# Twenty TensorE transpositions of the identity ahead of the first token tile

## The chip, the cores and the metric

The kernel runs on one core of a Trainium2 chip. A time is the device time of one execution in microseconds (us). The kernel before was timed three times: 1539.28, 1539.81 and 1539.98, median 1539.81. A fourth execution was recorded by the hardware profiler; all durations below are from it. PE is TensorE (matrix products and transpositions), PEld its weight loads, DVE is VectorE, ACT is ScalarE, POOL is GpSimd, SP is the engine that issues most DMAs.

## The reference

Eight sequences of 512 tokens with 512 features go through one block:

```python
xn = layernorm(x)
q, k, v = (xn @ W.T + b for W, b in ((Wq, bq), (Wk, bk), (Wv, bv)))
context = (elu(q) + 1) * cumsum((elu(k) + 1) * v, axis=1) * 32 ** -0.5
s = context @ Wo.T + bo
h = fwht(xn * SU_ug) / 64
h = silu(h @ W_gate.T * wg * 64) * (h @ W_up.T * wu * 64)
g = silu((fwht(h * SU_dp) / 64) @ W_down.T * wd * 64)
out = x + s * g
```

`fwht` is a normalized Walsh-Hadamard transform over the features; there are 2048 hidden features.

## The kernel before

The eight sequences are taken as four pairs. All matrices are float32. Every big product is a 2 by 2 block product done with seven products in place of eight; the seven operands are named P1 to P7, and their token side lies in one tile, `xo`, whose seven places are made by subtractions on DVE. The Hadamard transforms are folded into the weights on the chip, a first time through, by DVE butterflies and a PE product with the matrix `had` (tiles `pw`, `pwd`).

The first pair is special. Its token tiles x come in row by row, and `first_layernorms` (lines 157 to 185) normalizes eight tiles of 128 tokens: for each, DVE takes statistics (L173, L174) and adds epsilon (L175), ACT takes the root into `rs_first` (L176), DVE takes the reciprocal (L180), and then ACT scales the tile (L183, first four tiles) or DVE does (L185, last four). `transposed` (L271 to L289) then turns each tile with four PE transpositions into a PSUM bank `pt` (L276). For the first sequence ACT copies the bank into places P1 and P2 of `xo` (L280). For the second, ACT copies half of it into P3 (L283), and DVE makes P5, P6 and P7 from the bank and from places that are there already (L284 to L286). The bank pool has two buffers with the tag `t`, used in turn, so the third tile's transpositions wait until the first tile's bank has been read.

The products follow: `group` (L469) accumulates P1, P6, P5 and P3 in a bank px, P2 in py and P7, P4 in pz. For k of the first pair these are px_k with P1, py_k, px_k with P6, pz_k with P7, and so on. ACT takes snapshots of px (L481), and DVE adds (L485). The weights w_k, w_v, w_q are encoded in the same manner by DVE (L321 to L324) after their four parts have landed (L363), and are stored for later pairs (L335). The output projection uses w_o (loaded by L380), banks px_o, py_o, pz_o (L545).

The order on each engine is not the source's. A list scheduler with its own idea of how long instructions take, and with priorities in program order, places instructions one by one; each engine then works through its list strictly in order. Only the DVE part of `first_layernorms` is pinned in program order. So an instruction that is added ahead changes what the scheduler believes to be ready, and with that the order of others.

## Time and profile before

| what | value |
|---|---|
| median of three timed runs | 1539.81 us |
| profiled execution, its own time | 1539.19 us |
| its span, first to last instruction | 1537.4 us |
| PE busy | 1519.2 us (99%) |
| DVE busy | 1001.7 us (65%) |
| ACT busy | 419.6 us (27%) |
| first PE instruction | 7.22 us after the start |
| PE waits over 0.5 us after that | 2.17, 1.0, 0.65 and 0.63 us |

A line in a timeline gives the start, the duration, the engine, the source line, the operation, output and inputs, the count, and in brackets how long the engine was idle before it and what ended that. A line in the chain of waits gives the start, how long it set the pace, and what it was. In a table by stretches, each engine has its busy time and, in brackets, its number of instructions; the last three columns are the granted TensorE clock, the share of DMA and GB/s. The record of the granted clock starts with its first change, so stretches ahead of that show 1.00 whatever the clock was.

### The profile page before, as it was taken

To read this page: it belongs to the slowest core of one execution; us is meant where nothing else is said; L and a number is where in the kernel's file an instruction comes from. 1 tells how busy PE (TensorE), PEld (TensorE's weight loads), DVE (VectorE), ACT (ScalarE), POOL (GpSimd) and SP (SyncE) were. 2 spreads that over 40 slices of the span, in tenths; PEclk is the share of its full clock that TensorE was granted. 3 is DMA by queue.
4 is the path that set the end of the run, shared out by engine and by line. 5 is a ranking of instruction groups with operands and counts; after the bars stand their busy time and mean duration, and the time that the engine had idled before them with its cause. 6 is when DMAs were issued, how large, how long until landed. Compare 5 with 4: busy or idle time off the path is not lost.

```text
span 1537.4 us, 15667 instructions
## 1 busy us (share of the span) xinstructions
PE 1519.2 (99%) x5924; PEld 1121.8 (73%) x5924; DVE 1001.7 (65%) x1471; ACT 419.6 (27%) x664; POOL 345.0 (22%) x188
## 2 busy tenths in 40 slices
PE   7999999999999999999999999999999999999998
PEld 3446446748864688888884588888886478888887
DVE  8999787579775765426867674716675575633673
ACT  4462442232135311112114421111213431111211
POOL 1000000001221161107320153303611126200631
PEclk9999999999999999999999999999999999999999
DMA  8345888698965235254675344344574233525462
GB/s 283 94 142 178 265 276 252 215 321 276 273 236 145 100 119 188 86 193 147 198 268 191 88 165 151 106 143 166 195 235 152 72 120 107 191 93 179 163 257 82
DMA packets 197692, 273.31 MB, mean 178 GB/s; under 512 B 56816, under 2 KB 155120, under 8 KB 193392
## 3 DMA queue, kind: packets, MB, share of 16 engines
q1 hardware_dynamic: 197472, 272.27, 54.0%
q8 instruction: 47, 0.77, 0.2%
q14 instruction: 29, 0.24, 0.0%
q10 hardware_dynamic: 144, 0.03, 0.0%
HBM read 196.25 MB, written 76.02 MB: 177 GB/s over the span
## 4 chain that ended last, share of the span: by engine, by line
PE 92%; DVE 5%; DMA 1%; ACT 1%; issue 1%; POOL 0%; SPq 0%; POOLq 0%; DVEq 0%; ACTq 0%
PE px_gu L647 20%; PE px_dn L545 14%; PE pz_gu L647 10%; PE pz_dn L545 7%; PE py_gu L647 5%; PE py_dn L545 4%; PE px_o L545 3%; PE px_k L469 3%; PE px_q L469 3%; PE px_v L469 3%; PE px_gate L469 2%; PE px_up L469 2%; PE pz_o L545 2%; PE pz_v L469 2%; PE pz_k L469 2%; PE pz_q L469 2%
## 5 line engine op out<-in xcount | busy, mean ns | idle before, releaser
L647 PE MATMUL px_gu<-xo,w_gu 128*128 128x256 f32 x1456 | 347.4, 380 | 0.0
L647 PEld LDWEIGHTS px_gu<-xo,w_gu 128*128 128x128 f32 x1456 | 276.1, 190 | 43.9 <-issue 5.0
L545 PE MATMUL px_dn<-w_down,ho 128*128 128x256 f32 x1024 | 228.8, 379 | 1.0 <-DVE ho L93 1.0
L856 POOL TENSOR_TENSOR u<-u,v 128x1024 f32<-128x1024 f32 x26 | 61.2, 2374 | 721.7 <-DVE u L685 682.4
L545 PEld LDWEIGHTS px_dn<-w_down,ho 128*128 128x128 f32 x1024 | 194.6, 190 | 29.3 <-issue 1.9
L647 PE MATMUL pz_gu<-xo,w_gu 128*128 128x256 f32 x728 | 187.3, 380 | 0.0
L647 PEld LDWEIGHTS pz_gu<-xo,w_gu 128*128 128x128 f32 x728 | 137.8, 190 | 20.2 <-DVE a L689 0.9
L545 PE MATMUL pz_dn<-w_down,ho 128*128 128x256 f32 x496 | 112.4, 379 | 0.0
L545 PEld LDWEIGHTS pz_dn<-w_down,ho 128*128 128x128 f32 x496 | 93.9, 190 | 14.5 <-issue 1.2
L647 PE MATMUL py_gu<-xo,w_gu 128*128 128x256 f32 x364 | 93.4, 379 | 0.0
L901 POOL TENSOR_TENSOR s<-s,d 128x512 f32<-128x512 f32 x30 | 40.0, 1333 | 165.5 <-ACT d L900 165.5
L647 PEld LDWEIGHTS py_gu<-xo,w_gu 128*128 128x128 f32 x364 | 69.2, 190 | 9.4
L860 POOL TENSOR_TENSOR v<-v,r 128x1024 f32<-128x1024 f32 x26 | 60.8, 2362 | 27.2 <-DVE r L685 27.2
L469 PE MATMUL px_k<-xo,w_k 128*128 128x512 f32 x128 | 61.1, 600 | 0.0
L846 ACT ACTIVATE a<-a,cols_sb 128x512 f32<-128x512 f32 x26 | 18.7, 721 | 154.3 <-DVE a L685 152.7
L469 PE MATMUL px_v<-xo,w_v 128*128 128x512 f32 x128 | 60.6, 594 | 0.0
L469 PE MATMUL px_q<-xo,w_q 128*128 128x512 f32 x128 | 60.3, 592 | 0.0
L900 ACT ACTIVATE d<-d 128x512 f32<-128x512 f32 x31 | 19.5, 630 | 144.4 <-DVE d L560 124.7
L545 PE MATMUL px_o<-w_o,co 128*128 128x256 f32 x256 | 58.5, 380 | 0.2 <-DVE sa_o L556 0.2
L846 ACT ACTIVATE u<-u,cols_sb 128x512 f32<-128x512 f32 x52 | 36.9, 720 | 78.2 <-DVE u L685 75.0
L545 PE MATMUL py_dn<-w_down,ho 128*128 128x256 f32 x256 | 57.9, 379 | 0.0
L841 POOL TENSOR_TENSOR ho<-ho 128x1024 f32<-128x1024 f32 x24 | 56.3, 2355 | 1.4
(264 smaller groups left out, 2282.5 us busy)
## 6 DMA issues: line engine op xcount, KB each, us to landing
w_gu<-d_gu SPq DMA_DIRECT2D x91, 896.0 KB, 4.4
w_down<-d_down SPq DMA_DIRECT2D x56, 512.0 KB, 4.0
d_s<-o SPq DMA_DIRECT2D x8, 1024.0 KB, 6.0
d_d<-dn SPq DMA_DIRECT2D x8, 1024.0 KB, 7.6
d<-d_d SPq DMA_DIRECT2D x8, 1024.0 KB, 5.8
s<-d_s SPq DMA_DIRECT2D x8, 1024.0 KB, 7.7
y<-in_x_dram SPq DMA_DIRECT2D x8, 1024.0 KB, 6.9
out_dram<-y SPq DMA_DIRECT2D x15, 512.0 KB, 3.3
```

The lines of the kernel that those rows point to most:

```text
L469: nc.tensor.matmul(p.rearrange("p a t -> p (a t)") if len(r.shape) == 2 else p, ws[k][:, i, :], r, start=(first and k == 0), stop=(k == n ...
L545: nc.tensor.matmul(p[:, c], t[:, (2 * g + c) * P : (2 * g + c + 1) * P], ws[i](k), start=(first and k == 0 and c == cs[0]), stop=(k == n - ...
L647: nc.tensor.matmul(p[:, lane], w[:, lane, i, :], x[:, i, :], start=(first and lane == 0), stop=True, skip_group_check=True,)
L841: eng.tensor_tensor(ho[:, :, c], ho[:, :, a], ho[:, :, b], ALU.subtract)
L846: nc.scalar.activation(g[:, m], g[:, m], AF.Silu, scale=col("w_gate", u + m * NU + a * NG))
L856: nc.gpsimd.tensor_tensor(r[:, m], ru1[:, m], rv[:, m], ALU.add)
L860: nc.gpsimd.tensor_tensor(rv[:, m], rv[:, m], rr[:, m], ALU.add)
L900: nc.scalar.activation(d, d, AF.Silu)
L901: (nc.vector if final and (a, s) == (1, 0) else nc.gpsimd).tensor_tensor(r, r, d, ALU.mult)
```

## The change

After the identity matrix has been made, a PSUM tile `spare` with the tag `t` is taken, and PE transposes the identity into it twenty times. Nothing reads `spare`. The output does not depend on it. Since `spare` takes a buffer of the pool `t`, the first token tile's bank is now the other of the two.

```diff
     nc.scalar.dma_start(cols_sb, cols)
     make_identity(nc, ident)
+    spare = ps.tile([P, P], F32, tag="t", name="spare")
+    for _ in range(20):
+        nc.tensor.transpose(spare, ident, ident)
     had2 = t8.tile([P, P], F32, tag="t", name="had2")
```

## The prediction

> **What bounds the kernel now.** I read the page first, then the list of what PE waited for, then the chain of waits, then stretches of the first and last microseconds.

> ```profile
> span 1537.4 us, 15667 instructions
> ...
> PE   7999999999999999999999999999999999999998
> ```

> The list of PE's waits (who, for whom, total us, times, longest):

> ```profile
> PE pt L276 <- ACT x L183: 7.2, 1, 7.2
> PE pz_o L545 <- DVE g L485: 2.2, 1, 2.2
> PE px_dn L545 <- DVE ho L93: 1.0, 1, 1.0
> PE pz_k L469 <- DVE k L485: 0.2, 1, 0.2
> ```

> PE is the bound in all slices but the first and last, and its waits after the first 7.2 us are few. So whatever PE loses or gains in the first 23 us arrives at the end, unless one of those waits takes it up. The start itself, from the chain (start, how long it set the pace, what):

> ```profile
> 10.95 0.48 ACT xo L280
> 11.42 0.04 issue
> 11.47 1.97 PE pt L276 x8
> 13.44 2.39 PE px_k L469 x4
> 15.83 0.44 PE pt L276 x4
> 16.27 1.72 PE py_k L469 x4
> ...
> 23.16 1.92 PE px_k L469 x4
> ```

> Until 11.47 us the normalization on DVE and ACT sets the pace, then PE. Eight transpositions take 1.97 us there (1.79 from first start to the next product's start at 13.26, so 0.22 each); later four take 0.44, 0.11 each. The change of pace falls inside the first px_k, at about 14.5 us: before it PE ran at half speed. I call that the closed clock. The rows by stretches say when it opens and closes:

> ```profile
> 7.60:11.00 3.40, 2.63 (x12) 1.74 (x10) 3.12 (x13) 3.15 (x7) 0.00 (x0) 1.00 1.12 355
> 11.00:14.40 3.40, 3.23 (x12) 2.19 (x11) 3.36 (x12) 2.05 (x6) 0.00 (x0) 1.00 1.02 302
> ...
> 1530.00:1533.40 3.40, 1.62 (x8) 1.09 (x6) 2.69 (x6) 1.04 (x2) 0.00 (x0) 1.00 0.45 175
> 1533.40:1536.80 3.40, 0.00 (x0) 0.00 (x0) 0.87 (x3) 0.42 (x1) 0.00 (x0) 1.00 0.57 210
> 1536.80:1537.40 0.60, 0.00 (x0) 0.00 (x0) 0.00 (x0) 0.00 (x0) 0.00 (x0) 0.52 0.00 0
> ```

> PE busy is the first figure after the comma. A stretch with 2.63 of 3.40 busy did not open the clock, one with 3.23 did; one with 1.62 at the end did not close it, an empty one did (0.52 after 1536.8). So a nearly full stretch opens, and the share that closes lies somewhere between 0 and 48%.

> **The change, part by part.** All sums are against the profiled execution, 1539.19 us, which is 0.62 below the median of 1539.81.

> *The twenty transpositions.* They wait for the identity alone (POOL, done at 1.30). At 0.22 us each they end by 1.3 + 20 x 0.22 = 5.7 us. The first token tile is ready at 7.12, when PE starts at 7.22 in the profile. They cost nothing directly; the cover is this wait of 7.2 us, and without it they would cost 2.2 (open) to 4.4 us (closed).

> *The bank.* `spare` takes one of two buffers, and only PE writes it. The second token tile takes it over in PE's own order, so there is no new wait; the banks alternate as before. Zero.

> *The order on ACT and PE.* This is the part with a price. The changed program's order (where its instructions stand, not when) shows that the scheduler believes the token tiles to be turned later and puts ACT's copies (L280) behind more of the normalization. ACT had copy 0, scale 3, copy 1, root 5, copies 2 and 3, root 6. It will have scale 3, root 5, copy 0, root 6, copies 1, 2, 3, root 7. DVE's order is the same up to the last statistics. Root 6 is the trap, as these two rows show:

> ```profile
> 11.42 0.58 ACT L280 COPY xo<-pt 128x512 f32<-128x512 f32 x1
> ...
> 13.05 0.14 DVE L175 TENSOR_SCALAR rs_first<-mv_first 128x1 f32<-128x1 f32 x1
> ```

> Copies 1 and 2 began at 10.85 and 11.42; now they stand behind root 6, which needs the DVE result of 13.05 + 0.14. By the rows' durations: root 5 at 11.1, copy 0 to 11.85, root 6 13.25 to 13.45, copy 1 to 13.95, copy 2 to 14.45. PE turns tile 3 in the bank of copy 1 from 14.0, ACT copies it, PE turns tile 5 in that bank, and only then comes px_k, because PE's list now has tiles 4 and 5 ahead of it. With the clock open: tile 3 to 14.45, copy 3 from 14.6 to 15.2, tile 5 from 15.25 to 15.7, px_k from 15.7 to 17.4. Before, px_k plus the same six tiles were done at 16.1. Next, PE's list is py_k, tiles 6 and 7, px_v, half of py_v: 1.72 + 0.88 + 1.72 + 0.86 = 5.18, so px_k's second product starts at 22.6. DVE, which makes P6 for it, gets there at about 22.5: the root of tile 7 comes earlier (it stood behind the px_k snapshot, a DVE wait of 0.66 at 16.95), and four encodings of w_v move into that hole. In the profile this product started at 23.1, but with two half-products of 0.86 more behind it. So PE loses 22.6 + 1.72 - 23.1 = 1.2 us by order alone.

> *The clock at px_k.* It would have to be opened by the twenty (4.4 us dense) and stay open over the poor stretch that follows: tiles 0 to 2 at 7.2, 8.45 and 11.9, each 0.44, tile 3 at 14.0. A stretch of 3.4 us there holds about 0.44, or 13%. The rows leave 0 to 48% open; 13% is nearest to the empty row, which closed. I take it as closed. Then tile 3 takes 0.85, copy 3 runs 15.1 to 15.7, tile 5 ends at 16.6, and px_k starts 0.9 later than above. From 16.6 until the opening g, PE does half its work: (g - 16.6)/2. The bounds of g: the dense work began at 11.47 in the profile and opened 3.0 later, so 14.0 + 3.0 = 17.0; or from PE's first instruction, 7.3 us, so 14.0 + 7.3 = 21.3. The opening also came only 1.2 us after the first matrix product (13.26), so the row can't say if transpositions count; by that count g is 17.8. I take 18.5, nearer the dense row: 0.95 us.

> [...]

> *What takes it up or adds.* The PE wait of 0.2 us for k (67.5) goes: -0.2. The wait of 2.2 us of pz_o does not help, since the chain runs through PE to it:

> ```profile
> 102.28 1.73 PE px_gate L469 x4
> 104.01 0.20 SPq L380
> ...
> 105.61 3.71 DMA w_o<-in_wo_t_dram
> ```

> PE frees the weight buffer at 104.0, w_o lands at 109.3, DVE had waited 2.0 us for it and is busy from there to 134.8. If PE is late at 104, all of it is late. In the new order two 256-wide px_o products (0.43 together, as eight of py_o took 1.73) move from ahead of that wait to behind it: +0.43. The wait of 1.0 us at 240 hangs on pw_up of PE at 218 through two transfers, so it moves along.

> *SP, ACT and DVE later.* The store of w_k moves ahead of the last load of the next w_k, which lands some 1.5 us later, for a reader at 25.0 (its landing takes 4.0): hidden. The second load of rd moves behind the store of w_v; its reader is at 40.8. The load of bo_r moves ahead of w_v's second load by 0.4 us of issue. Around 170 us the store to wd_f moves behind two loads, and one of eight reads back (0.7 us of issue) ahead of the s_up stores; rd is read at 190.6. sa_up moves behind two groups of pwd scalings on ACT, whose product px_up moved as well. POOL's order is the same. I put all these at zero; uncovered, each would cost up to its issue, 0.4 to 0.7 us.

> Sum: 1.2 + 0.9 + 0.95 - 0.2 + 0.43 = 3.3, so 1539.19 + 3.3 = 1542.5 us, 0.17% over the median.

> **The rivals.**

> *Open at px_k.* The twenty open the clock and 13% keeps it open. 1.2 - 0.2 + 0.43 = 1.4: 1540.6 us. For it: 48% kept it open. Against: a stretch of 13%.

> *Late opening: slower.* One mechanism, the clock opening at px_k and after. The base with opening at 16.6 is 1539.19 + 1.2 + 0.9 - 0.2 + 0.43 = 1541.5; 1542.9 is passed if g is over 19.3, and 21.3 gives 1543.9; its middle, 20.3, gives 1543.4. It decides if only matrix products count and the stretches fall badly.

> *The change does what it says: faster.* Clock open and the copies no trap: 4.36 us of the chain (1.97 + 2.39) would be 0.88 + 1.72 = 2.60, so 1.76 less, 1537.4. To pass 0.2% the wait of 2.17 us must go too: 1535.3. Against it: P6 on DVE was ready only at 23.1 anyway, and the order above.

> **How the numbers follow.** About 0.2% (3.1 us) is what a measurement can tell from no change. Closed with g up to 19.3: 0.38, no change. Open: 0.22, no change. Late opening: 0.35, slower. A gain past 0.2%: 0.05. So 0.05, 0.60 and 0.35. The range goes from 1540.2 (the open case less 0.4 for a moved transfer) to 1544.2 (g of 21.3 plus 0.3).

> **What would show it.** In the profile after: 20 transpositions between 1.3 and 5.8 (right if PE's first wait shrinks to 1.3); copy 1 of L280 after 13.3; px_k from 15.7 (open) or 16.6 (closed); four transpositions taking 0.85 or 0.44 at 14.0; px_k's second product at 22.6 or later; the wait of pz_o at 136 to 139 with about 2 us. If the copies are not late, or the pz_o wait shrinks by a microsecond, the sum is wrong.

## The result and the profile after

The changed kernel took 1543.28 us (median of 22 executions, 1540.84 to 1544.36), the kernel before on the same chip 1539.49 (22 executions). The ratio is 1.002, with a 95% interval of 1.0014 to 1.0026: slower by about 3 us by the ratio, while the medians lie 3.79 apart. The executions of the changed kernel fall into two groups, twelve from 1543.18 to 1544.36 with a mean granted clock of 0.995 and ten from 1540.84 to 1542.60 with 0.996 to 1.0; both profiles of it, here and in the repeated run below, are of the upper group. The profiled execution took 1543.74 us, 4.55 more than that of before (1539.19). The page of the changed kernel:

```profile
span 1542.0 us, 15704 instructions
...
PE   8999999999999999999999999999999999999998
...
PEclk8999999999999999999999999999999999999999
```

PE's first digit is 8 in place of 7, since the twenty transpositions fill the old wait, and the clock's first digit is 8 in place of 9. The list of PE's waits (who, for whom, total us, times, longest):

```profile
PE pt L276 <- ACT xo L280: 3.7, 2, 2.7
PE pz_o L545 <- DVE g L485: 2.2, 1, 2.2
PE pt L276 <- ACT x L183: 2.0, 2, 1.4
PE spare L1162 <- POOL ident masks.py:199: 1.4, 1, 1.4
...
PE px_dn L545 <- DVE ho L93: 0.5, 1, 0.5
```

The first wait of 7.2 us has become 1.4 and 1.4 us, and a new one stands at the top: 3.7 us in which PE waits for ACT's copies. The timeline shows it (start, duration, engine, line, operation, output and inputs, count; in brackets the idle time before and what ended it):

```profile
1.36 4.39 PE L1162 MATMUL spare<-ident 128*128 128x128 f32 x20 [1.36 <-POOL ident masks.py:199]
...
7.11 0.66 PE L276 MATMUL pt<-ident,x 128*128 128x128 f32 x4 [1.36 <-ACT x L183]
...
11.81 1.12 PE L276 MATMUL pt<-ident,x 128*128 128x128 f32 x4 [2.74 <-ACT xo L280]
...
13.18 0.20 ACT L176 ACTIVATE rs_first<-rs_first 128x1 f32<-128x1 f32 x1 [1.42 <-DVE rs_first L175]
13.29 1.05 ACT L280 COPY xo<-pt 128x512 f32<-128x512 f32 x2
...
13.91 2.91 PE L276 MATMUL pt<-ident,x 128*128 128x128 f32 x12 [0.98 <-ACT xo L280]
...
16.61 3.14 PE L469 MATMUL px_k<-xo,w_k 128*128 128x512 f32 x4
```

Copies 1 and 2 begin at 13.29, right behind root 6 at 13.18; px_k begins at 16.61 in place of 13.26. The first four transpositions of a token tile take 0.66 us, those at 11.81 take 1.12: the clock was open and closed again. The table by stretches (busy time of PE, PEld, DVE, ACT, POOL with instructions in brackets, then granted clock, DMA share, GB/s):

```profile
5.40:8.80 3.40, 1.42 (x11) 0.92 (x9) 3.09 (x16) 2.24 (x6) 0.52 (x2) 1.00 1.05 367
8.90:12.30 3.40, 0.66 (x5) 0.50 (x4) 3.19 (x12) 2.40 (x5) 0.00 (x0) 0.50 1.15 343
12.30:15.70 3.40, 2.42 (x12) 1.79 (x11) 3.40 (x15) 1.80 (x5) 0.00 (x0) 0.50 0.50 147
15.70:19.10 3.40, 3.40 (x8) 1.92 (x8) 3.39 (x11) 0.79 (x3) 0.00 (x0) 0.50 0.97 283
...
135.10:138.50 3.40, 1.23 (x6) 0.78 (x5) 3.40 (x4) 0.50 (x1) 0.00 (x0) 1.00 1.15 344
138.60:142.00 3.40, 3.40 (x10) 2.69 (x9) 3.40 (x7) 0.55 (x1) 0.00 (x0) 0.50 0.09 28
```

The trace's record of the clock has it open from 5.48 us, half from 8.89, open from 19.13, and then, which the prediction did not have, half again from 138.59 to 142.01. These changes and the closing at the end (1541.47) lie multiples of 3.413 us apart: 1, 4, 39, 40 and 450 times 3.413 behind the first. I call such a stretch of 3.413 us a window. In before, the clock opened at 14.48 us and stayed open until 1536.82, 446 times 3.413 later and behind PE's last product.

Where the 4.55 us come from can be followed on PE, by the start of the same matrix product in both profiles. At px_k's second product PE starts at 24.75, 1.64 later than before (23.11), with 1.72 us of products moved behind it: 3.36 us late. At pz_o behind the wait of 2.17 us it is 138.02 against 135.55, 2.47 late, with four px_o products of 0.86 moved behind it: 3.33. From 145 us on, where the order is nearly the same, PE is 5.01 late: the second closing has added 1.68. The wait of px_dn at 240 us gives 0.47 back, since it is 0.5 in place of 1.0. That leaves 4.54.

### The profile page after: what moved, and what is told of

Read it like the earlier page. It is cut to its first block, busy times and chain, and to the rows that moved or that the text cites. A ratio compares the mean times of both kernels' runs of the same rounds, so it can differ in the third digit from the quotient of the medians.

```text
span 1542.0 us, 15704 instructions
## 1 busy us (share of the span) xinstructions
PE 1524.9 (99%) x5944; PEld 1126.4 (73%) x5944; DVE 1003.3 (65%) x1471; ACT 420.1 (27%) x664; POOL 345.1 (22%) x188
## 4 chain that ended last, share of the span: by engine, by line
PE 91%; DVE 5%; DMA 1%; ACT 1%; issue 1%; POOL 0%; SPq 0%; POOLq 0%; DVEq 0%; ACTq 0%
PE px_gu L647 20%; PE px_dn L545 14%; PE pz_gu L647 10%; PE pz_dn L545 7%; PE py_gu L647 5%; PE py_dn L545 4%; PE px_o L545 4%; PE px_k L469 3%; PE px_v L469 3%; PE px_q L469 3%; PE px_gate L469 2%; PE px_up L469 2%; PE pz_o L545 2%; PE pz_k L469 2%; PE pz_v L469 1%; PE pz_q L469 1%
## 5 line engine op out<-in xcount | busy, mean ns | idle before, releaser
L545 PE MATMUL px_dn<-w_down,ho 128*128 128x256 f32 x1024 | 228.8, 379 | 0.5 <-DVE ho L93 0.5
L545 PEld LDWEIGHTS px_dn<-w_down,ho 128*128 128x128 f32 x1024 | 194.5, 190 | 29.0 <-issue 1.9
L647 PEld LDWEIGHTS pz_gu<-xo,w_gu 128*128 128x128 f32 x728 | 137.7, 190 | 20.3 <-DVE a L689 0.9
L545 PE MATMUL pz_dn<-w_down,ho 128*128 128x256 f32 x496 | 112.4, 379 | 0.0
L545 PEld LDWEIGHTS pz_dn<-w_down,ho 128*128 128x128 f32 x496 | 93.8, 190 | 14.6 <-issue 1.2
L469 PE MATMUL px_k<-xo,w_k 128*128 128x512 f32 x128 | 61.7, 605 | 0.0
L469 PE MATMUL px_v<-xo,w_v 128*128 128x512 f32 x128 | 60.4, 594 | 0.0
L469 PE MATMUL px_q<-xo,w_q 128*128 128x512 f32 x128 | 60.1, 592 | 0.0
L545 PE MATMUL px_o<-w_o,co 128*128 128x256 f32 x256 | 59.0, 381 | 0.0
L545 PE MATMUL py_dn<-w_down,ho 128*128 128x256 f32 x256 | 57.9, 379 | 0.0
```

What stands on the lines that cost most here:

```text
L469: nc.tensor.matmul(p.rearrange("p a t -> p (a t)") if len(r.shape) == 2 else p, ws[k][:, i, :], r, start=(first and k == 0), stop=(k == n ...
L545: nc.tensor.matmul(p[:, c], t[:, (2 * g + c) * P : (2 * g + c + 1) * P], ws[i](k), start=(first and k == 0 and c == cs[0]), stop=(k == n - ...
L647: nc.tensor.matmul(p[:, lane], w[:, lane, i, :], x[:, i, :], start=(first and lane == 0), stop=True, skip_group_check=True,)
```

## The experiments

All the experiments but the changed kernel itself fix the order. A helper of 39 lines gives each engine a list of the positions of its first instructions (205 on ACT, 327 on DVE, 116 on SP, 291 on PE) and chains them by dependences for the scheduler alone, without a wait on the chip. The list is that of before ("early") or that of the changed kernel ("late"). With the helper, L280 is L319, L469 is L508 and L545 is L584. Its core:

```diff
+    for engine, places in ORDER.items():
+        mine = [i for i in bb.instructions if i.engine.name == engine and i.name not in extra ...]
+        chain = [mine[p] for p in places]
...
+        for i, j in zip(chain[1:], chain):
+            tc.add_manual_dep(i, j.name, DependencyInfo(NoSync, DATA), reason="as_listed")
```

### The order without the twenty, and the twenty without the order

Theory: the new order costs, the transpositions themselves are free. Rival: the transpositions cost, through the clock or the bank. The first kernel has the late lists and no transpositions:

```diff
     make_identity(nc, ident)
-    spare = ps.tile([P, P], F32, tag="t", name="spare")
-    for _ in range(20):
-        nc.tensor.transpose(spare, ident, ident)
...
+    as_listed(tc, extra, ())   # ORDER: the changed kernel's
```

> The lists of all engines are those of the changed kernel, but the twenty transpositions are left out. Theory O (the order costs, the twenty themselves do nothing lasting): copy 1 (L280) begins after 13.2 us, px_k at about 16.6 us with the clock closed, its second product at 24.3 to 25.2 us in place of 23.1, and the time is that of the changed kernel within 1 us, 1542 to 1544. Theory C (the clock that the twenty open and lose again costs, the order little): without them the clock opens as before at 14.5 to 17 us, and the time is 1539.5 to 1541.

Measured: 1543.77 us against 1540.07 of before on that chip, ratio 1.0022 (1.0013 to 1.0031). The whole loss is there without a single added transposition. px_k begins at 16.67, its second product at 24.11, a little ahead of the 24.3 to 25.2 that was expected:

```profile
16.67 2.43 PE L508 MATMUL px_k<-xo,w_k 128*128 128x512 f32 x4
```

The second has the twenty and the early lists:

```diff
+    spare = ps.tile([P, P], F32, tag="t", name="spare")
+    for _ in range(20):
+        extra.add(nc.tensor.transpose(spare, ident, ident).ins.name)
...
+    as_listed(tc, extra, ())   # ORDER: that of before
```

> The twenty transpositions, with all engines' lists as in the kernel before. Theory O: the twenty open the clock at 5 to 8 us and lose it again, px_k begins at 13.3 us or earlier, its second product at 23.1 us within 0.4, time 1539.5 within 0.7. Theory C: the clock lost at about 9 us opens later than the 14.5 us of before, and the time is 1541 to 1542.

Measured: 1539.84 us, ratio 0.9999 (0.999 to 1.0008). The twenty cost nothing, and they gain nothing: in the profile they open the clock at 4.76 us, it closes at 8.17 and opens again at 15.00, half a microsecond later than in the profile of before, and px_k begins at 13.27. Two of the eleven executions lie higher, at 1542.55 and 1543.57, with a mean clock of 0.995 where the other nine have 0.997 or 0.998; they have no profile.

### One instruction put back

The changed kernel, with only root 6 moved in ACT's list behind copies 1, 2 and 3:

```diff
-    "Activation": [..., 10, 13, 11, 14, 15, 16, 12, 17, ...],
+    "Activation": [..., 10, 13, 14, 15, 16, 11, 12, 17, ...],
```

> The changed kernel with one instruction moved on ACT: root 6 behind copies 1, 2 and 3 in place of ahead of them. If root 6 is what makes the copies late: copy 1 at 11.8 us, px_k at about 15.2 us in place of 16.6, time 1541 to 1542.2. If the cost lies in PE's list (tiles 4 and 5 ahead of px_k): 1543 to 1543.7 as before the move.

Measured: 1540.18 us, ratio 1.0004 (0.9996 to 1.0013), below both of the expected ranges. One root of 128 numbers, moved by three places, takes back most of the loss: nearly all of it by the median, and all but some 0.6 us by the ratio. Six of the eleven executions lie at 1539.91 to 1540.18, the other five 2 us higher, at 1542.05 to 1542.25; the profile is of the lower group, and why the five are slower is not shown. The table by stretches and the timeline of this kernel show how:

```profile
12.30:15.70 3.40, 3.40 (x18) 2.80 (x17) 3.40 (x15) 1.49 (x6) 0.00 (x0) 0.62 0.67 179
15.70:19.10 3.40, 3.37 (x12) 1.34 (x10) 3.40 (x12) 1.59 (x4) 0.00 (x0) 1.00 0.96 276
```

```profile
11.88 3.44 PE L315 MATMUL pt<-ident,x 128*128 128x128 f32 x16 [2.31 <-ACT xo L319]
...
15.16 1.88 PE L508 MATMUL px_k<-xo,w_k 128*128 128x512 f32 x4
```

PE turns four tiles without a gap from 11.88 on, so one window is nearly full (2.98 of 3.41 us busy) and the clock opens at 14.86, ahead of px_k. In the changed kernel the gap until 13.91 breaks that window (2.42 of 3.40 us busy in the stretch from 12.30); the clock opens only at 18.39 to 19.13 in its two profiles, and most of px_k runs in the closed clock.

### The clock held open, order of before

Can the clock be worth something by itself? Here transpositions fill PE's gaps from 1.4 us to px_k, with the early lists:

```diff
-    for _ in range(20):
-        nc.tensor.transpose(spare, ident, ident)
+    spare = bank("px", "spare", 2)[:, 0, :P]
+    for ahead_of, n in ((0, 28), (4, 6), (8, 10), (12, 6)):
+        filler(ahead_of, n, spare)   # n transpositions ahead of PE's listed instruction
```

> Lists as in the kernel before, with 28 transpositions of the identity ahead of tile 0 and 6, 10 and 6 more behind tiles 0, 1 and 2, so that PE has no poor stretch before px_k. If the closed clock at the start has a price on the path: open from 8.2 us at the latest without closing, px_k at 12.6 us and done by 14.4, 1538.4 to 1539.0. If DVE sets the second product of px_k anyway: it stays at 23.1 us and the time at 1539.5. If the fillers get in the way of the tiles: 1540 or more.

Measured: 1539.15 us, ratio 0.9994 (0.9985 to 1.0003). In the profile, of the fastest of the eleven executions (1537.91), PE is 1.03 us ahead of before at px_k's second product and from 145 us on. The same kernel once more on another chip:

> The order of the kernel before with the clock held open from 7 us through px_k, once more: the only kernel so far below the kernel before (1539.15 against 1540.07, ratio 0.9994 with an interval that holds 1). Theory C (px_k in the open clock gains 1.03 us at 25 us and nothing takes it up): 0.8 to 1.3 us below the kernel before, the load of w_gate at 242 us takes 3.2 us, and PE waits for nothing at 246 to 253 us. Rival D (the gain is lost to a slower load of w_gate at 242 us, as in the kernel with both fillings, where it took 5.3 us and PE waited 2.2): within 0.5 us of the kernel before or above it, with a wait of pz_dn at about 251 us.

Measured: 1540.83 us against 1540.85, ratio 1.0 (0.9991 to 1.0009). In this profile PE is 0.71 us ahead at px_k's second product, but the clock closes for a window at the wait of pz_o (135.77 us), and from 145 us on PE is 1.01 late. So there is a gain at px_k in the profiles, and no kernel here that can be told from before to its good.

### The second closing

First the changed kernel once more:

> The changed kernel once more, on the chip of the next three. All theories: 3 to 4 us over the kernel before, in two groups some 2.3 us apart, the lower one with a mean clock above 0.995. It is the base for what the next three take back.

Measured: 1543.83 us (7 executions), 1539.56 for before, ratio 1.0026 (1.0015 to 1.0037). Six executions lie at 1543.24 to 1544.72 with a mean clock of 0.995; one lies at 1541.22 with 0.999. The mean clock alone doesn't tell which execution closed a second time, since its record starts with the first change: the run with the late lists and no transpositions has 0.999 in its profile and closes at 137.23. Then sixteen more transpositions just ahead of pz_o, in PE's wait of 2.2 us:

```diff
+                if name == "o_0" and g == 1:
+                    filler(None, 16, bank("t", "spare_o", 2)[:, 0, :P])
                 product(pz[g], P7, g, True, ks)
```

> The changed kernel in its own order, with sixteen more transpositions of the identity into a bank that nobody reads, placed in PE's list just ahead of the first pz_o product of the second group, where PE waits 2.2 us for DVE. Theory C (the second closing of the clock at 138.6 us is a term of its own, 3.4 us at half speed, 1.7 us, in most runs): PE is busy through the wait, the clock stays at 1.00 from 135 to 142 us in the profile, no run has the mean clock 0.995, and the median falls by 1.4 to 2.0 us against the changed kernel, to 1.2 to 2.0 over the kernel before. Rival W (the wait of pz_o is what costs, the clock only happens to fall there, or DVE sets the pace behind it): the median stays within 0.6 us of the changed kernel. Rival F (the sixteen run past the end of the wait): slower by 0.1 to 1 us, with pz_o starting behind the last of them.

Measured: 1541.93 us, ratio 1.0016 (1.0007 to 1.0025), 1.90 under the changed kernel, and no execution with a mean clock of 0.995. It is 2.37 over before, more than the 1.2 to 2.0 expected. The changed kernel's timeline (the repeated run), and then the filled one:

```profile
134.02 1.46 PE L545 MATMUL px_o<-w_o,co 128*128 128x256 f32 x6
137.64 3.61 PE L545 MATMUL pz_o<-w_o,co 128*128 128x256 f32 x8 [2.16 <-DVE g L485]
```

```profile
134.09 1.46 PE L584 MATMUL px_o<-w_o,co 128*128 128x256 f32 x6
135.39 1.91 PE L1202 MATMUL t_spare_o<-ident 128*128 128x128 f32 x16
137.72 1.99 PE L584 MATMUL pz_o<-w_o,co 128*128 128x256 f32 x8 [0.41 <-DVE g L524]
```

pz_o starts at the same time (137.64 and 137.72), but its eight products take 1.99 in place of 3.61 us. So the wait itself is DVE's and is not shortened; what costs 1.6 us is the half clock behind it. Theory C holds, W and F fall.

### The clock at px_k, and the order by itself

The late lists with the clock held open through px_k:

```diff
+    for ahead_of, n in ((0, 28), (4, 6), (8, 24), (12, 14)):
+        filler(ahead_of, n, spare)
```

> The changed kernel in its own order, with 28 transpositions in place of the 20 ahead of tile 0, and 6, 24 and 14 more ahead of tiles 1, 2 and 3, so that PE is busy from 1.4 to 15 us and the clock is open at px_k. It prices the clock at px_k. Theory S (the sum of the prediction: 0.9 us of a later start and 0.95 to 1.3 us at half speed): px_k starts at about 15.7 in place of 16.6 and its four matrix products take 1.9 in place of 3.1 us; PE is 1.8 to 2.2 us ahead of the changed kernel at px_k's second product (24.8 there); the total falls by as much where the second closing stays as it is, and by up to 3.9 where it goes as well. Rival D (DVE's P6 for the second product and the w_o load set the pace anyway): px_k is early, its second product comes no earlier than 24 us, and the total falls by less than 0.8 us.

Measured: 1542.98 us, ratio 1.0022 (1.0013 to 1.0032), 0.85 under the changed kernel. The timeline of this kernel, and of the repeated run of the changed one:

```profile
15.80 1.88 PE L508 MATMUL px_k<-xo,w_k 128*128 128x512 f32 x4
...
22.69 1.88 PE L508 MATMUL px_k<-xo,w_k 128*128 128x512 f32 x4
```

```profile
16.66 2.75 PE L469 MATMUL px_k<-xo,w_k 128*128 128x512 f32 x4
...
24.41 1.88 PE L469 MATMUL px_k<-xo,w_k 128*128 128x512 f32 x4
```

At the second product PE is 1.72 ahead: the price of the clock there, which theory S put at 1.8 to 2.2. The median gives only half of it back, and rival D's sign (a second product no earlier than 24) did not show. Two things can account for the rest. The profile is of the fastest of the ten executions (1541.71); in it PE is 1.23 us late against before at 235 us and 2.51 at the end, so 1.3 us are lost behind 235 us (below). And six of the ten executions, 1542.82 to 1544.49, have a mean clock of 0.998 where the four faster ones have 0.999, which fits a second closing; that is argued from the next run, where the wait of pz_o is filled too, no execution has 0.998 and the median is 1.50 lower. With both fillings:

```diff
+    for ahead_of, n in ((0, 28), (4, 6), (8, 24), (12, 14)):
+        filler(ahead_of, n, spare)
...
+                    filler(None, 16, bank("t", "spare_o", 2)[:, 0, :P])
```

> Both fillings in one kernel: the order of the changed kernel with the clock open at px_k and through the wait of pz_o. What is left over the kernel before is the price of the order by itself: by the prediction's terms 1.2 - 0.2 + 0.43 = 1.4 us, so 0.8 to 2.0 over the kernel before with the second theory of no clock cost at all (rival: the order alone is worth all of the loss) giving 3 to 4. If it is within 0.5 us of the kernel before, root 6 costs nothing while the clock is open, and the whole loss was the clock's.

Measured: 1541.48 us, 1.9 over before, ratio 1.0012 (1.0003 to 1.002). In its profile PE is 1.27 us late from 145 us on, near the 1.4 of the prediction's terms; the remainder of the total lies in waits behind 235 us. Once more:

> The run with both fillings once more, for the same chip as the two before. If the waits behind 235 us (0.6 us of pz_dn at 252, 1.1 us of pz_gu at 360, both behind loads) come of PE being early, they show again here and the median is again 1.5 to 2.3 over the kernel before; if they were chance, they are gone from the profile and the median is 0.8 to 1.4 over it, which is what the prediction's terms of order give (1.4).

Measured: 1541.37 us against 1539.41, ratio 1.0012 (1.0003 to 1.002). The wait of pz_dn at 252 us (0.6) is there again, that of pz_gu (1.1) is gone. And root 6 put back, with both fillings:

```diff
-    "Activation": [..., 10, 13, 11, 14, 15, 16, 12, 17, ...],
+    "Activation": [..., 10, 13, 14, 15, 16, 11, 12, 17, ...],
...
+    for ahead_of, n in ((0, 28), (4, 6), (8, 24)):
+        filler(ahead_of, n, spare)
```

> The order of the changed kernel with ACT's root 6 put back behind copies 1, 2 and 3, the clock held open through px_k and through the wait of pz_o. Beside the run with the same fillings and root 6 in its new place (1541.48, 1.9 over the kernel before) it prices root 6 with the clock out of the account. Theory O (root 6 delays px_k by more than a microsecond in any clock): px_k starts near 13.5 in place of 15.8, and the total is 1.5 to 2.5 us lower, so from 0.6 under to 0.4 over the kernel before. Rival K (root 6 cost only because it put px_k into the closed clock): the total stays within 0.6 us of 1.9 over the kernel before.

Measured: 1540.69 us, ratio 1.0009 (1.0 to 1.0018), 0.68 under the run with root 6 in its new place. px_k begins at 14.67, since DVE's scaling of tile 5 now sets the pace (PE waits 0.35 us for it ahead of 14.20) and PE's late list has that tile ahead of px_k, and its second product at 22.32 in place of 22.70:

```profile
14.67 1.88 PE L508 MATMUL px_k<-xo,w_k 128*128 128x512 f32 x4
...
22.32 1.88 PE L508 MATMUL px_k<-xo,w_k 128*128 128x512 f32 x4
```

So with the clock open root 6 is worth 0.4 us at the second product and 0.68 between the medians, though the intervals of the two ratios overlap; theory O (1.5 to 2.5) falls. Rival K, which had 0.6 as its bound, comes near: most of what root 6 costs, it costs through the clock.

### The order of before with both fillings, and the waits behind 235 us

```diff
+    for ahead_of, n in ((0, 28), (4, 6), (8, 10), (12, 6)):
+        filler(ahead_of, n, spare)
...
+                    filler(None, 16, bank("t", "spare_o", 2)[:, 0, :P])
```

> The order of the kernel before, the clock held open from 5 us through px_k (28, 6, 10 and 6 transpositions ahead of tiles 0, 1, 2 and 3) and sixteen more through the wait of pz_o. The candidate to beat both kernels. Theory C (the clock's closings are worth 1.3 us at px_k and 1.7 us in each execution that closes again at the wait of pz_o): 1.0 to 1.6 us under the kernel before, with no execution more than 1.5 us over the median, and none below a mean clock of 0.999. Rival D (behind 235 us the loads of the weights set DVE's pace, and PE waits for it longer when it is early): PE is as far ahead at 145 us, but its waits behind 235 us grow by 0.5 us or more, and the total is within 0.6 us of the kernel before.

Measured: 1540.54 us against 1539.41, ratio 1.0009 (1.0 to 1.0018): the candidate is a microsecond slower in the median, at the edge of what can be told apart. The profile is of the third slowest of the eleven executions (1542.31), so it shows how the gain can be lost, and more than the median lost. In it PE is 1.03 ahead of before at px_k's second product and 1.01 ahead from 145 us on; then the gain is lost, and PE is 3.01 late from 256 us on. DVE's waits of this kernel between 225 and 256 us, then PE's:

```profile
DVE s_up L460 <- DMA d_gu<-s_gate: 4.1, 1, 4.1
DVE w_gate L999 <- DMA w_gate<-in_wgate_t_dram: 2.4, 1, 2.4
```

```profile
PE pz_dn L584 <- DVE u L524: 2.2, 1, 2.2
...
PE px_dn L584 <- DVE ho L132: 0.9, 1, 0.9
```

The load of w_gate takes 5.3 us there (median from issue to landing); DVE waits for it with pz_dn's operand queued behind it, PE waits 2.2 us for that, and the clock closes once more, from 252.03 to 255.45 us. The wait that rival D foresaw is there; its total, within 0.6 us of before, is missed by 0.5.

But being early isn't its whole cause. The load took 4.2 to 5.3 us in six of the seven profiles with the clock held open at the start, 3.2 in the seventh (the first run of the early lists with the clock held), and 3.1 to 3.2 in the seven profiles without. In two of these last, root 6 put back and the early lists with the twenty, PE comes to 235 us within 0.4 us of five of the six slow ones. What slows it was not found.

## Why the prediction was right or wrong

The forecast of 1542.5 us lies 0.8 under the median of 1543.28, inside the range. The sum had a term missing, which both profiles of the changed kernel show, and a smaller one that it put at nothing. That the number came so near is in part luck. Over the profile of before the sum has 3.3 us and the profile after 4.55; the missing 1.68 is partly hidden by 0.47 that came back at 240 us. And the forecast lies between the two groups of executions, under the median of 22 only because twelve of them are in the upper one.

- **The twenty transpositions, and the bank: zero.** Right. They run from 1.36 to 5.75 us, and with the order of before the time is 0.9999 of before.
- **The order: 1.2 us.** Right in size. With the clock held open and the late lists, PE is 22.69 + 1.72 - 23.11 = 1.30 late at px_k's second product. Copy 1 was forecast after 13.3, behind root 6, and came at 13.29. But root 6 is the smaller part of these 1.30: with it put back and the clock held open, 22.32 + 1.72 - 23.11 = 0.93 stay, which root 6 doesn't explain; which of the other moves they belong to was not taken apart. What root 6 costs lies mostly in the next term.
- **Closed at px_k: 0.9 + 0.95.** Right, and it decides between the first two cases, though the clock closed a window earlier than the argument had it: at 8.89 us, behind a window that was 42% busy, and not in the stretch of 13%. px_k was forecast at 16.6 and came at 16.61; the clock opened at 19.13 in one profile and 18.39 in the other, for 18.5. The price at px_k's second product was 24.41 - 22.69 = 1.72 us in the repeated run and 24.75 - 22.69 = 2.06 in the first profile (1.85 forecast). What the prediction's row could not say, if transpositions count, the profile after shows: twenty of them alone opened the clock at 5.48 us, ahead of any other product of PE.
- **0.2 for pz_k, and the w_o chain that passes everything on.** The sum came through to the wait: 3.05 - 0.2 + 0.43 = 3.28 was forecast, and PE was 3.33 late there for equal work (2.96 in the repeated run). That is two misses that cancel: pz_o started 2.47 later and not 2.85, and four px_o products had moved behind the wait and not two (0.86, not 0.43). And the wait of 2.17 us ended otherwise than the prediction had it. The chain of waits of the changed kernel:

```profile
134.26 3.57 DMA w_up<-in_wup_t_dram
...
138.02 3.25 PE pz_o L545 x8
141.27 0.85 PE px_o L545 x2
```

  DVE stood behind the landing of w_up, not behind w_o. That the wait kept its length was right.
- **What failed: the share of a window that closes the clock, "somewhere between 0 and 48%", was applied to the start only.** The wait of 2.17 us stood in the prediction as a wait that moves along unchanged. It was not asked what share of a window it leaves busy. It leaves 36%, and the clock closed: 1.68 us in the profile (5.01 - 3.33), 1.90 between the medians with and without filling.
- **The wait of 1.0 us at 240 "moves along".** Mis-sized: it shrank to 0.5, 0.8 and 0.3 in the three profiles of the changed kernel and its filled form, and so gave back 0.47 in the first of them.
- **The rivals.** Open at px_k fell: the clock was closed from 8.89 us on. Late opening, beyond 19.3, did not occur: 19.13 at the latest. But a forecast of up to 1543.9 came true by another route, the second closing. Faster fell: the open clock gains 0.7 to 1.0 us at px_k and nothing that the time shows.

Two things are argued rather than shown. One is why the changed kernel closes the second time in most executions and the kernel before in few. The table gives the idle part of the wait of pz_o that lies in one window, from the record of the clock (its first opening plus multiples of 3.413 us) and PE's timeline:

| kernel | wait | window | idle inside | closed behind it |
|---|---|---|---|---|
| before | 133.38 to 135.55 | 133.94 to 137.36 | 1.61 | no |
| changed | 135.85 to 138.02 | 135.18 to 138.60 | 2.17 | yes |
| changed, repeated | 135.48 to 137.64 | 134.44 to 137.86 | 2.16 | yes |
| late lists, no twenty | 135.19 to 137.34 | 133.81 to 137.23 | 2.04 | yes |
| early lists, twenty | 133.66 to 135.83 | 134.47 to 137.88 | 1.36 | no |
| root 6 back | 133.44 to 135.61 | 134.33 to 137.74 | 1.28 | no |
| late lists, held | 133.76 to 135.91 | 132.03 to 135.45 | 1.69 | no |
| early lists, held, first run | 132.34 to 134.51 | 133.05 to 136.46 | 1.46 | no |
| early lists, held, second run | 132.70 to 134.87 | 132.36 to 135.77 | 2.17 | yes |

Idle of 2.04 us or more of this wait in a window closed the clock in each case, 1.69 or less in none. The windows fall differently in each of these profiles; the change moves the wait by 2.1 to 2.5 us against them. Why they so often cover it whole afterwards was not settled. The other is the slow load of w_gate.

## What to carry to other kernels

Work added to an idle engine can be free and still cost: look at what it does to the lists that a scheduler makes, above all where a small instruction that waits for another engine is put ahead of a copy that PE waits for. When a stretch moves, ask of each short wait behind it which share of a clock window it leaves busy: here a wait of 2.2 us that left 36% cost another 1.7 at half clock. And price such a step on the chip by pinning the order: the order without the work, and the work without the order, told in two runs what the trace could not.
